# Sorting inside a graph network kernel: one vector product a step sooner, and two row-number operations moved between the halves of a one-hot matrix

## The chip, the cores and the metric

The kernel runs on one core of a Trainium2 chip, in one launch. The metric is the device time of an execution in microseconds (us). The core's engines work side by side, each through its own list of instructions in order: PE (matmuls, with PEld loading their weights), DVE (vector operations), ACT (activations and copies), POOL (here mostly indirect DMAs), and SP, which issues DMAs. An instruction that needs another engine's result waits on a semaphore, and all that stands behind it on its engine waits with it.

## The reference

A graph of 12,500 nodes with 64 features and 200,000 edges, sorted by destination. Two layers of neighbour means, then a network over the edges whose messages are averaged at the edge's source:

```
h = max(layernorm(x), 0)
for (Wl, Wr, b), relu in ((layer 1, yes), (layer 2, no)):
    agg  = segment_sum(h[src], dst)            # over 200,000 edges
    mean = agg / max(count(dst), 1)
    h    = mean @ Wl.T + b + h @ Wr.T          # relu after the first
x = x + h
h = max(layernorm(x), 0)
m = relu(concat(h[src], h[dst], edge) @ W1 + b1) @ W2 + b2
x = x + segment_sum(m, src) / max(count(src), 1)
```

## The kernel before, in words

The nodes are cut into 49 blocks of 256 (two nodes in each of 128 partitions). Every pair of a source block and a destination block is a cell, so there are 49 x 49 = 2401 cells with at most 128 edge slots each. Gathering and summing are matmuls with one-hot matrices, cell by cell. For that, the edges of every destination block have first to be sorted into their cells. This is the work of `sort(B)`, which is the place of the change.

**The sort of one block.** A block's window of edges lies as 128 partitions x 34 edges. `kv` says for each edge which source block it belongs to; `slo` and `dlo` are the local numbers (1 to 256) of its source and destination node inside their blocks. The sort runs in 13 steps (`STEPS = 13`; each `yield` ends one):

- step 1: DVE makes the one-hot matrix of source blocks, `v[:, :, 0]` (line 570, 1666 elements in each partition; the tile is called `hot3`, and `hot` in the profile).
- step 2: 34 small matmuls count the edges of each cell (line 575).
- step 3: DVE makes the running sums and `wide` (lines 579 to 582), and then comes the first of the four matmul steps.
- steps 4 to 6, with the rest of step 3, are a loop of four passes, n = 0 to 3: PE multiplies a piece of `v` (lines 591 and 592), and ACT copies the result into `ranks` (line 593). In passes 1 and 3 DVE also makes one product each (line 595): `v[:, :, 1]` = one-hot x `slo` in pass 1, and `v[:, :, 2]` = one-hot x `dlo` in pass 3. These products are the weights of the matmuls of line 619, four to five steps later.
- step 7: DVE takes minima over `ranks` (line 600 twice, line 603) and so gets each edge's rank in its cell, `rank`, and a rounded copy `rank_b` (line 605). Line 600 reads what ACT wrote in all four passes.
- steps 8 and 9: DVE makes the one-hot matrix of slots in two halves, `hot_r` (line 610, 2304 and 2048 elements in each partition).
- steps 10 and 11: PE multiplies the first half (18 matmuls) and the second half (16 matmuls) with the two products (line 619). Step 10 ends with two small DVE operations (lines 624 and 625, 34 elements in each partition) that work out `pos`, the rows of a table in memory to which POOL later scatters the edges' terms (line 370).
- steps 12 and 13: ACT copies the sums to `rows_o` (line 628); three DMAs write them out (lines 632 to 634), one of them to `srow_b`, which the layers read; PE and ACT turn them into `scol` and `dcol`.

**What runs around it.** The first block is sorted alone. From then on the steps of `sort` are dealt out between the groups of four cells of layer 1 (`sort_to`), about one step to a group once three blocks are ahead. A group gathers its cells (PE line 849, weights `turned`), copies them (ACT line 853, `rows`), and three groups later sums them (PE line 729, weights `hot`). DVE makes `turned` from `srow`, which SP loads, two operations to 16 cells (line 695), and one `hot` to a group (line 704, five buffers). At the end of each block's 49 cells comes `conv` (lines 770 to 794). From cell 150 on, the terms of the edges run beside it (`edge_terms`, lines 359 to 409, and POOL's scatter in line 370).

The order of instructions on each engine is that in which the Python code issues them; nothing reorders them. Tiles with one buffer are `v`, `wide`, `ranks`, `rank` and the bank `pX`; `kv`, `slo`, `dlo` and `hot_r` have two.

Of the kernel before, what the change touches and what calls it, by code (L numbers as in the profile page):

```python
# [9 lines left out]
FT = mybir.dt.float32  # L10
# [3 lines left out]
OP = mybir.AluOpType  # L14
AX = mybir.AxisListType
P = 128
# [98 lines left out]
def fast_path(  # L115
# [18 lines left out]
    nc = tc.nc  # L134
# [5 lines left out]
    NB = -(-N // BLK)  # L140
# [9 lines left out]
    T = 34  # L150
# [3 lines left out]
    S = P  # L154
# [14 lines left out]
    def table_of(B):  # L169

        if B < EARLY:
            return B % J, BJ, B // J
        i, j = divmod(B - EARLY, LJ)
        return J + j, len(range(j, LATE, LJ)), i
# [309 lines left out]
    def pos_of(B):  # L484
        return pos[:, B] if B < EARLY else pos_late[:, B - EARLY]
# [3 lines left out]
    def made_cells(work, psum):  # L489
# [61 lines left out]
        def pairs(a):  # L551
            return a.rearrange("p (g c) -> p g c", c=2)

        def mid(a, n):

            return a.unsqueeze(2).to_broadcast([a.shape[0], a.shape[1], n, 2])

        def lead_(a, n):

            return a.unsqueeze(1).to_broadcast([a.shape[0], n, a.shape[1], 2])  # L560

        def flat(a):
            return a.rearrange("p g k c -> p g (k c)")

        def sort(B):

            kv, slo, dlo = batch[B]

            v = work.tile([P, TG, 3, NB, 2], BF, name="hot3", bufs=1)
            nc.vector.tensor_tensor(v[:, :, 0], mid(pairs(kv), NB), lead_(kexp, TG), op=OP.is_equal)  # L570
            yield
            many = psum.tile([P, 512], FT, name="pX")
            for g in range(TG):
                for c in range(2):
                    nc.tensor.matmul(many[:NB, 2 * g + c:2 * g + c + 1], v[:, g, 0, :, c], ones[:, 0:1],  # L575
                                     start=True, stop=True)
            yield
            b = before[B % 2]
            nc.vector.tensor_tensor_scan(b[:, 1:T + 1], flat_ones, many[:NB, :T], 0.0, op0=OP.mult, op1=OP.add)
            w = work.tile([NB, TG, NB, 2], BF, name="wide", bufs=1)  # L580
            nc.vector.tensor_mul(w, mid(pairs(b[:, 0:T]), NB), lead_(own[:NB], TG))
            nc.vector.tensor_max(most, most, b[:, T:T + 1])


            r = work.tile([P, TG, NB, 2], BF, name="ranks", bufs=1)
            for n, g0 in enumerate(range(0, TG, 5)):
                yield
                g1 = min(g0 + 5, TG)
                p = psum.tile([P, 512], FT, name="pX")
                q = p[:, :(g1 - g0) * 2 * NB].rearrange("p (g k) -> p g k", k=2 * NB)  # L590
                nc.tensor.matmul(q, lead, flat(v[:, g0:g1, 0]), start=True, stop=False)
                nc.tensor.matmul(q, ones[:NB], flat(w[:, g0:g1]), start=False, stop=True)
                nc.scalar.copy(flat(r[:, g0:g1]), q)
                if n % 2:
                    nc.vector.tensor_mul(v[:, :, 1 + n // 2], v[:, :, 0], mid(pairs((slo, dlo)[n // 2]), NB))
            yield
            k = NB
            for _ in range(2):
                h = k - k // 2
                nc.vector.tensor_tensor(r[:, :, 0:k - h], r[:, :, 0:k - h], r[:, :, h:k], op=OP.min)  # L600
                k = h
            rank = work.tile([P, T], FT, name="rank", bufs=1)
            nc.vector.tensor_reduce(pairs(rank), r[:, :, 0:k].rearrange("p g k c -> p g c k"), AX.X, OP.min)
            rb = work.tile([P, T], BF, name="rank_b", bufs=1)
            nc.vector.tensor_scalar(rb, rank, float(S), None, op0=OP.add)
            halves = []
            for g0, g1 in ((0, (TG + 1) // 2), ((TG + 1) // 2, TG)):
                yield
                hot = work.tile([P, (TG + 1) // 2, S, 2], BF, name="hot_r")
                nc.vector.tensor_tensor(hot[:, :g1 - g0], mid(pairs(rb)[:, g0:g1], S), lead_(rexp, g1 - g0),  # L610
                                        op=OP.is_equal)
                halves.append((g0, g1, hot))
            p = psum.tile([P, 512], FT, name="pX")
            for g0, g1, hot in halves:
                yield

                for g in range(g0, g1):
                    for c in range(2):
                        nc.tensor.matmul(p[:2 * NB, :S], v[:, g, 1:3, :, c].rearrange("p v k -> p (v k)"),  # L619
                                         hot[:, g - g0, :, c], start=g + c == 0, stop=g + c == TG)  # L620
                if g0 == 0:
                    j, n, f = table_of(B)
                    q = work.tile([P, T], FT, name="pos_f", bufs=1)
                    nc.vector.scalar_tensor_tensor(q, rank, float(NB), kv, op0=OP.mult, op1=OP.add)
                    nc.vector.tensor_scalar(pos_of(B), q, float(n), float(n * (S * NB + NB) + f),
                                            op0=OP.mult, op1=OP.add)
            o = work.tile([2 * NB, S], BF, name="rows_o")
            nc.scalar.copy(o, p[:2 * NB, :S])
            yield
            n, f = place[B]  # L630
            F = len(order[n])
            nc.sync.dma_start(srow_b[B].rearrange("(k s) -> k s", s=S), o[0:NB])
            nc.sync.dma_start(srow_k[n][:, f * S:(f + 1) * S], o[0:NB])
            nc.sync.dma_start(drow_k[n][:, f * S:(f + 1) * S], o[NB:2 * NB])
            p = psum.tile([P, 512], FT, name="pX")
            pt = p.bitcast(BF)[:, 0:2 * NB]
            nc.tensor.transpose(pt, o, ident_b[:2 * NB, :2 * NB])
            nc.scalar.copy(scol[:, scol_at[n]:scol_at[n] + NB * F].rearrange("p (k f) -> p k f", f=F)[:, :, f],
                           pt[:, 0:NB])
            nc.scalar.copy(dcol[:, B * NB:(B + 1) * NB], pt[:, NB:])  # L640
            yield
# [4 lines left out]
        for B in range(NB):  # L646
            if B % CH == 3 and B + 4 < NB:
                coming = edges_in(B + 4, nc.sync)
            for _ in sort(B):
                next(coming, None)  # L650
                sorted_to[0] += 1
                yield
# [108 lines left out]
    work = layers.enter_context(tc.tile_pool(name="layers", bufs=2))  # L761
# [169 lines left out]
    work = ctx.enter_context(tc.tile_pool(name="last", bufs=2))  # L931
# [451 lines left out]
```

## Time and profile before

| what | value |
|---|---|
| median of 3 runs | 5045.93 us (5045.0 to 5051.07) |
| the profiled execution, its own time | 5056.79 us |
| its span, first to last instruction | 5055.0 us |
| mean granted clock of TensorE | 0.898 |
| first `ranks` to last `rows_o` (all sorting) | 121.8 to 1945.9 us of the span |
| 300 to 1950 us: PE / PEld / DVE / ACT / POOL busy | 1339.6 / 1146.2 / 978.7 / 716.9 / 913.4 us of 1650 |
| 300 to 1950 us: granted clock | 0.86 |
| 3600 to 4500 us: granted clock | 1.00 |

A group's row gives engine, line, operation, the tile written and the tiles read, the number of instructions, their time in sum and the mean of one in ns, and the engine's idle time before them with what ended it. In a timeline row come the start, the length, the engine and line, and in brackets how long the engine had been idle and what released it. "issue" is a wait for nothing that the profile shows. Four cells of a layer give eight matmuls each on lines 849 and 729.

### The profile page before, as it was taken

The numbers are of one execution on the slowest core, as the hardware profiler recorded it, in microseconds if no ns is written. First come the engines' busy times: TensorE is split into PE (matmuls) and PEld (weight loads), VectorE is DVE, ScalarE is ACT, GpSimd is POOL, SyncE is SP. The second block draws the span as 40 slices with busy tenths as digits, with TensorE's granted clock in tenths as the row PEclk, the third lists the DMA queues.
The fourth block names the chain that finished last, engine by engine and source line by source line (L and its number), as shares of the span: only waits on it lengthen the run. The fifth ranks groups of instructions, "written<-read, shape, count | busy, mean of one in ns | idle before, by whom it ended". The sixth has DMA issues, their size and how long they took to land.

```text
span 5055.0 us, 125955 instructions
## 1 busy us (share of the span) xinstructions
PE 4085.5 (81%) x50387; PEld 3709.4 (73%) x50387; DVE 3404.9 (67%) x5945; ACT 2592.5 (51%) x5894; POOL 2682.8 (53%) x2299
## 2 busy tenths in 40 slices
PE   0778887878878888787887787777899999999866
PEld 0666776666766776777777777776899999999865
DVE  5655655555655655555555555555899999999986
ACT  2333444444444444444454444444677777777643
POOL 2035555545655645544554454443577777776532
PEclk9888888888888888888899898888999999999987
DMA  8843222222222222322323222223566666665653
GB/s 304 300 150 97 79 71 76 66 72 76 74 75 79 81 70 81 98 83 91 93 92 96 88 91 89 85 92 92 195 199 207 196 193 191 199 189 183 185 157 96
DMA packets 382102, 635.58 MB, mean 126 GB/s; under 512 B 97555, under 2 KB 236951, under 8 KB 381425
## 3 DMA queue, kind: packets, MB, share of 16 engines
q1 hardware_dynamic: 318116, 572.31, 35.8%
q0 software_dynamic: 53312, 51.36, 3.5%
q8 instruction: 396, 6.49, 0.5%
q10 hardware_dynamic: 10076, 3.77, 0.3%
q14 instruction: 202, 1.65, 0.1%
HBM read 474.72 MB, written 155.83 MB: 125 GB/s over the span
## 4 chain that ended last, share of the span: by engine, by line
PE 62%; issue 11%; DVE 10%; ACT 5%; POOL 3%; DMA 3%; another core or an unknown queue 3%; SPq 1%; ACTq 1%; DVEq 0%; POOLq 0%
PE acc L729 21%; PE got L849 17%; PE got L1025 7%; PE pE L401 4%; PE got L1026 3%; PE pX L619 2%; DVE turned L695 2%; DVE turned_d L695 2%; POOL hidden L1036 2%; PE pE L389 2%; ACT rows L853 2%; DVE hot L704 1%; POOL terms L370 1%; PE pX L575 1%
## 5 line engine op out<-in xcount | busy, mean ns | idle before, releaser
L370 POOL DMA_INDIRECT terms<-terms_o,pos x1496 | 1697.7, 1135 | 1706.0 <-ACT terms_o L409 693.9
L853 ACT CAST rows<-got 128x384 bf16<-128x384 f32 x2402 | 1076.0, 488 | 1680.2 <-PE got L849 962.3
L729 PEld LDWEIGHTS <-hot 128*128 128x128 bf16 x12012 | 1113.6, 105 | 269.0 <-issue 229.6
L729 PE MATMUL acc<-rows,hot 128*128 128x193 bf16 x9604 | 1162.8, 265 | 119.9 <-issue 114.9
L849 PEld LDWEIGHTS <-turned 128*128 128x128 bf16 x9604 | 892.2, 104 | 295.4 <-issue 276.9
L1036 POOL TENSOR_TENSOR hidden<-hidden 128x512 f32<-128x512 f32 (+1 forms) x602 | 768.1, 1276 | 531.9 <-ACT hidden L1033 450.0
L695 DVE TENSOR_SCALAR turned<-srow,nid 128x2048 bf16<-128x2048 bf16 (+1 forms) x906 | 775.5, 870 | 239.7 <-PE got L849 116.4
L704 DVE TENSOR_TENSOR hot<-dcol,local 128x1024 bf16<-128x1024 bf16 x1202 | 807.3, 684 | 56.7 <-PE acc L729 23.5
L1025 PE MATMUL got<-tb,turned_d 128*128 128x128 bf16 x4802 | 753.4, 223 | 28.4 <-DVE turned_d L695 27.0
L1025 PE MATMUL got<-ta,turned 128*128 128x128 bf16 x4802 | 744.8, 223 | 20.4 <-DVE y L1030 13.1
L1026 PE MATMUL got<-tb,turned_d 128*128 128x64 bf16 x4802 | 685.3, 195 | 0.0
L1026 PE MATMUL got<-ta,turned 128*128 128x64 bf16 x4802 | 678.9, 195 | 0.0
L849 PE MATMUL got<-tb,turned 128*128 128x192 bf16 x4802 | 574.9, 262 | 109.7 <-issue 89.9
L849 PE MATMUL got<-ta,turned 128*128 128x192 bf16 x4802 | 577.5, 264 | 85.6 <-issue 74.4
L1044 ACT ACTIVATE hot_a<-every,less 128x256 bf16<-128x256 bf16 x1197 | 507.7, 496 | 0.0
L1025 PEld LDWEIGHTS <-turned_d 128*128 128x128 bf16 x4802 | 449.6, 100 | 38.0 <-DVE turned_d L695 37.3
L1025 PEld LDWEIGHTS <-turned 128*128 128x128 bf16 x4802 | 452.6, 100 | 8.2 <-issue 7.8
L1026 PEld LDWEIGHTS <-turned 128*128 128x128 bf16 x4802 | 446.0, 99 | 16.8 <-issue 15.3
L1026 PEld LDWEIGHTS <-turned_d 128*128 128x128 bf16 x4802 | 447.0, 99 | 0.0
L1033 ACT ACTIVATE hidden<-y 128x512 f32<-128x512 f32 (+1 forms) x301 | 190.1, 632 | 308.3 <-DVE y L1030 291.3
L1045 ACT ACTIVATE hot_a<-hot_a 128x1024 bf16<-128x1024 bf16 x300 | 316.9, 1056 | 9.5
L401 PE MATMUL pE<-we,edges_t 128*128 128x128 f32 x1666 | 291.4, 317 | 32.7 <-issue 30.3
(212 smaller groups left out, 5237.6 us busy)
## 6 DMA issues: line engine op xcount, KB each, us to landing
srow<-srow_b SPq DMA_DIRECT2D x300, 512.0 KB
srow<-srow_k SPq DMA_DIRECT2D x149, 512.0 KB
drow<-drow_k SPq DMA_DIRECT2D x149, 512.0 KB
terms<-tb SPq DMA_DIRECT2D x96, 704.0 KB
edges<-in_edge_attr_dram SPq DMA_DIRECT2D x235, 192.0 KB
terms_in<-terms SPq DMA_DIRECT2D x74, 352.0 KB
terms<-terms_o,pos POOLq DMA_INDIRECT x1496
sums_mem<-sums SPq DMA_DIRECT2D x49, 193.0 KB
```

Of the source, the lines that this page charges most:

```text
L370: nc.gpsimd.indirect_dma_start(out=terms[j][:], out_offset=bass.IndirectOffsetOnAxis(ap=pos_of(B)[:, t:t + 1], axis=0), in_=o[:, c, h], in ...
L401: nc.tensor.matmul(pm[:, c], et[:, c], we, start=True, stop=True)
L695: nc.vector.tensor_scalar(o[:, h, :n * S], r[:, :n * S], nid[:, h:h + 1], None, op0=OP.is_equal)
L704: nc.vector.tensor_tensor(o[:, :n], cols.rearrange("p (g c) -> p g c", c=2).unsqueeze(2).to_broadcast([P, n, 2 * P, 2]), local.rearrange(" ...
L729: nc.tensor.matmul(self.acc[B][:, h, :W3], lt, r[:, c, 0:W3], start=k + h == 0, stop=k == row - 1 and h == 1, skip_group_check=True)
L849: nc.tensor.matmul(p[:, (i - c) * D3:(i - c + 1) * D3], t[:, h, (a - c0 + i) * S:(a - c0 + i + 1) * S], table[:, (a + i) % NB, h], start=h ...
L853: nc.scalar.copy(g[:, c:c + m, :D3], p[:, :m * D3].rearrange("p (c d) -> p c d", c=m))
L1025: nc.tensor.matmul(p[:, c], lt, rt[:, 0:2 * D], start=i == 0, stop=False, skip_group_check=True)
L1026: nc.tensor.matmul(p[:, c, 0:D], lt, rt[:, 2 * D:], start=False, stop=i == 3, skip_group_check=True)
L1036: nc.gpsimd.tensor_sub(w[:, :n, (i + 1) * D:(i + 2) * D], w[:, :n, j], upper(w)[:, :n, j])
L1044: nc.scalar.activation(q[:, c - k], every, AF.Abs, bias=less[:, a - c0 + c:a - c0 + c + 1])
L1045: nc.scalar.activation(q[:, :n - k], q[:, :n - k], AF.Relu, bias=1.0, scale=-2.0)
```

## The change

Two edits in `sort`, both of which move DVE operations; the number, the shapes and the operands of the operations stay as they are.

```diff
                 nc.scalar.copy(flat(r[:, g0:g1]), q)
-                if n % 2:
-                    nc.vector.tensor_mul(v[:, :, 1 + n // 2], v[:, :, 0], mid(pairs((slo, dlo)[n // 2]), NB))
+                if n in (1, 2):
+                    nc.vector.tensor_mul(v[:, :, n], v[:, :, 0], mid(pairs((slo, dlo)[n - 1]), NB))
```

The product with `dlo` is issued in pass 2 instead of pass 3.

```diff
             for g0, g1 in ((0, (TG + 1) // 2), ((TG + 1) // 2, TG)):
                 yield
                 hot = work.tile([P, (TG + 1) // 2, S, 2], BF, name="hot_r")
                 nc.vector.tensor_tensor(hot[:, :g1 - g0], mid(pairs(rb)[:, g0:g1], S), lead_(rexp, g1 - g0),
                                         op=OP.is_equal)
                 halves.append((g0, g1, hot))
+                if g0 == 0:
+                    j, n, f = table_of(B)
+                    q = work.tile([P, T], FT, name="pos_f", bufs=1)
+                    nc.vector.scalar_tensor_tensor(q, rank, float(NB), kv, op0=OP.mult, op1=OP.add)
+                    nc.vector.tensor_scalar(pos_of(B), q, float(n), float(n * (S * NB + NB) + f),
+                                            op0=OP.mult, op1=OP.add)
             p = psum.tile([P, 512], FT, name="pX")
             for g0, g1, hot in halves:
                 yield

                 for g in range(g0, g1):
...
-                if g0 == 0:
-                    j, n, f = table_of(B)
-                    q = work.tile([P, T], FT, name="pos_f", bufs=1)
-                    nc.vector.scalar_tensor_tensor(q, rank, float(NB), kv, op0=OP.mult, op1=OP.add)
-                    nc.vector.tensor_scalar(pos_of(B), q, float(n), float(n * (S * NB + NB) + f),
-                                            op0=OP.mult, op1=OP.add)
```

The two row-number operations are issued in step 8, right behind the first half of `hot_r`, instead of at the end of step 10. In the changed kernel they are lines 616 and 617, and the matmuls of line 619 are line 625.

The order of PE, ACT, POOL and SP instructions is the same in both programs. On DVE the framework that places the semaphores puts 37 more separate waits in front of `hot` (line 704: 13 before, 50 after), each on a DVE operation ten or more instructions back; PE's weight loads for line 619 carry 9 waits fewer (12 before, 3 after).

## The prediction

> **What bounds the kernel now.** I read the page first, then the waits and the timeline of the stretch in which sorting runs.
>
> ```profile
> span 5055.0 us, 125955 instructions
> PE 4085.5 (81%) x50387; PEld 3709.4 (73%) x50387; DVE 3404.9 (67%) x5945; ACT 2592.5 (51%) x5894; POOL 2682.8 (53%) x2299
> PEclk9888888888888888888899898888999999999987
> PE 62%; issue 11%; DVE 10%; ACT 5%; POOL 3%; DMA 3%; another core or an unknown queue 3%; SPq 1%; ACTq 1%; DVEq 0%; POOLq 0%
> ```
>
> The chain that ended last is PE's for 62% and "issue" for 11%; the change touches DVE only. All of it lies between 117 and 1946 us, where a DVE operation costs time only if PE (or ACT, for PE) stands waiting for it. So I asked who waits, from 300 to 1950 us (columns: total us, times, longest):
>
> ```profile
> DVE ranks L600 <- ACT ranks L593: 87.2, 29, 7.6
> DVE ranks L600 <- ACT rows L853: 20.9, 9, 3.6
> DVE ranks L600 <- issue: 20.1, 5, 6.0
> PE pX L619 <- issue: 38.2, 68, 2.2
> PE pX L619 <- DVE hot_r L610: 2.0, 3, 1.2
> ```
>
> These 43 blocks make DVE stand 128 us in front of line 600, 3 us each: it has done its products long before ACT has copied the last ranks. PE, on its side, stands 2.0 us in total for the slots' matrix. The timeline of block 24 on DVE shows the order that the change rewrites:
>
> ```profile
> 1020.00 1.01 DVE L595 TENSOR_TENSOR hot<-hot,slo 128x1666 bf16<-128x1666 bf16 x1
> 1020.93 1.37 DVE L704 TENSOR_TENSOR hot<-dcol,local 128x1024 bf16<-128x1024 bf16 x2
> 1022.22 1.02 DVE L595 TENSOR_TENSOR hot<-hot,dlo 128x1666 bf16<-128x1666 bf16 x1
> 1024.23 0.75 DVE L695 TENSOR_SCALAR turned<-srow,nid 128x2048 bf16<-128x2048 bf16 x1 [0.99 <-PE got L849]
> 1024.90 0.68 DVE L704 TENSOR_TENSOR hot<-dcol,local 128x1024 bf16<-128x1024 bf16 x1
> 1027.04 0.99 DVE L600 TENSOR_TENSOR ranks<-ranks 128x816 bf16<-128x816 bf16 x2 [1.45 <-ACT ranks L593]
> ...
> 1031.72 2.49 DVE L610 TENSOR_TENSOR hot_r<-rank_b,rexp 128x2304 bf16<-128x2304 bf16 x2
> 1034.14 0.68 DVE L704 TENSOR_TENSOR hot<-dcol,local 128x1024 bf16<-128x1024 bf16 x1
> 1034.74 0.18 DVE L624 SCALAR_TENSOR_TENSOR pos_f<-rank,kv 128x34 f32<-128x34 f32 x1
> 1034.96 0.18 DVE L625 TENSOR_SCALAR pos<-pos_f 128x34 int32<-128x34 f32 x1
> 1035.05 0.69 DVE L704 TENSOR_TENSOR hot<-dcol,local 128x1024 bf16<-128x1024 bf16 x1
> ```
>
> **The product a step sooner.** One operation of 1.02 us in each of 49 blocks goes in front of up to two operations that stood before it, a `hot` or a `turned`. What it could win: line 600 starts sooner. It cannot, where DVE stands before it for ACT. Going through all 49 blocks, the first line 600 had an idle DVE in front of it in 48, and never less than 1.2 us. ACT's copies and PE's matmuls of those passes do not wait for the products, so line 600 stays and the idle time grows by the 1.02 us. The one block without idle time is block 4 (line 600 at 229.72). There line 605 ends at 231.57, the next operation is a `turned` that waits 3.46 us for the DMA of `srow` until 235.03, and swallows the 1.02. Gain: 0; bounds 0 to 1.02 us.
>
> What it could lose: the operations that now stand behind it come up to 1.02 us later. I took for each `hot` and `turned` between the two products the time from its end to the start of the first matmul that uses it. The smallest are 1.69, 1.71 and 2.42 us, all in block 4; the next is 4.9 us. A `hot` is summed three groups later, and that is the cover. All exceed 1.02, so the loss is 0. If the cover were gone, it would be 49 x 1.02 = 50 us.
>
> **The two row-number operations.** In a row of DVE work they take 1035.05 - 1034.74 = 0.31 us from the start of the first to the start of what follows. Alone they take more: in block 0 the first starts at 131.16 and the second, which waits for it, ends at 131.57, 0.41 us. I take 0.31, since the halves stand in a row with them, and keep 0.41 as the other end. In step 8 they push back the second half of `hot_r` and the groups' operations up to their old place. Cover of the second half: the time from its end to the first of its 16 matmuls. Over the 49 blocks this is 4.5 us in the median and below 0.41 us only in block 2 (end 172.33, matmuls at 172.40: 0.07 us); next come 0.47 (block 17) and 0.87 (blocks 0 and 1). So PE loses 0.31 - 0.07 = 0.24 us once, by the other end 0.34. The `turned` and `hot` in between have at least 1.08 us to their first matmul, more than 0.41. The operations behind the old place gain 0.31, and nobody waits for them. `pos` is ready sooner; the scatter that reads it waits for ACT's `terms_o` (429.8 us from 300 to 1950) and not for `pos`. Block 2's 0.24 us may vanish in the next wait for `srow`, so its bounds are 0 and 0.34.
>
> **Waits and queues.** SP, POOL, PE and ACT have the same order; no DMA is moved. The 37 added waits of DVE ask for DVE operations at least ten instructions old; the separate waits of line 704 in the trace last 21 ns each, together 0.8 us on an engine that idles 3 us a block in front of line 600. Behind such a wait stands the `hot` itself, with the slack above. Cost 0, bound 0.8.
>
> **Sum.** On the span of 5055.0 (execution 5056.79, so 1.79 outside): 0 + 0.24 + 0 = +0.2. That execution is 10.9 us over the median of the runs, so I add to the median: 5045.93 + 0.24 = 5046.2. Bounds of the costs: -1.0 (block 4) to +1.1 (0.34 + 0.8).
>
> A rule that speaks against this: in the profile the granted clock is 0.86 from 300 to 1950 us and 1.00 from 3600 to 4500, where PE is 96% busy. The Trainium skill, "TensorE: Matmul & The Clock Gate" (What's actually happening), says that the array drops to half clock after a quiet window of about 3.4 us, and that the windows run free. By the row, a PE wait of 0.24 us costs 0.24; by the rule it could tip a window and cost about 1.7 us more (an estimate, half of that page's 3.4). Either stays below what can be told.
>
> **Rivals.** *No change* (the forecast), 5046.2.
>
> *Slower: the second half becomes what PE waits for.* The place is the first matmul of step 11, the price 0.31 us a block, 49 x 0.31 = 15.2, so 5061 (by 0.41: 5066). It decides from the point where the second half's slack is below 0.31; for 10 us that must be so in 33 blocks. For it: PE stands for the first half (slack about 0.05 to 0.1) in 16 blocks, so DVE is late there, and the pair follows at once. Against it: a group of layer work separates the halves' matmuls, and only block 2 is that tight.
>
> *Faster: the slots' matrix comes sooner.* If line 600 were held by DVE's own work, the first half would be ready 1.02 us sooner. PE stands before it in 14 blocks: 3.69, 3.44, 0.76, 7.18, 2.17, 0.47, 0.03, 0.10, 1.21, 0.32, 0.54, 0.10, 0.10 and 1.18 us. Cut at 1.02 each, that is 8.5 us, so 5037. Against it: the idle time before line 600.
>
> *The stalls fall differently.* The clock of 0.86 takes 0.14 x 1650 = 231 us of full-clock time; "issue" stalls of PE lie in the same stretch. A shift of DVE by a microsecond can rearrange which loads meet which matmuls. A twentieth of 231 us is 12 us, either way: 5034 or 5058. For it: the stalls are large. Against it: the three runs agree within 6 us. *That the change does nothing on DVE* is out: the built order shows both moves.
>
> **How the numbers follow.** Within about 0.2% (10 us) two versions of this kernel can't be told apart. Forecast 0.60. Second half late 0.13. Slots' matrix sooner 0.07, of which 0.03 goes beyond 0.2% with help from the stalls. Stalls rearranged 0.20, of which I give 0.10 to faster, 0.09 to slower and 0.01 to the middle. So faster 0.13, same 0.60 + 0.04 + 0.01 = 0.65, slower 0.22. The likeliest case's own range is 5040 to 5052: its bounds and the 6 us spread of the runs. For 8 in 10 the range takes in the lighter rearrangements and most of the second-half case: 5034 to 5062.
>
> **What would show it.** In the profile after: the second product directly behind pass 2; DVE's idle time before line 600 up by about 1 us a block (154 us over all blocks before, some 200 after); the pair between the halves at 0.31 to 0.41 us; the second half's slack 0.3 to 0.4 us smaller while PE's idle time before its matmuls stays near nothing; granted clock 0.86 in the same stretch. I am wrong if PE stands before the second half in many blocks, if PE's waits for `hot` or `turned` rise from next to nothing, or if clock and "issue" between 300 and 1950 us differ by more than 10 us.

## The result, and the profile after

The changed kernel takes 5075.62 us (median of 20 runs, 5033.91 to 5119.84), beside 5048.43 us (5035.76 to 5075.13, 20 runs) for the kernel before. The ratio is 1.0052, with a 95% interval of 1.0031 to 1.0073; two runs of the changed kernel, 5111.3 and 5119.84 us, count as slow and are left out of it. It is slower by half a per cent, 27 us between the medians, and above the end of the predicted range. The profiled execution took 5091.81 us. On the page of the changed kernel (span, busy time by engine, granted clock in 40 slices, the chain that ended last):

```profile
span 5090.0 us, 125992 instructions
PE 4096.7 (80%) x50387; PEld 3720.7 (73%) x50387; DVE 3402.1 (67%) x5945; ACT 2584.0 (51%) x5894; POOL 2676.0 (53%) x2299
PEclk9878888888888888888988898898899999999987
PE 61%; issue 14%; DVE 9%; ACT 5%; POOL 4%; DMA 3%; another core or an unknown queue 3%; ACTq 1%; SPq 1%; POOLq 0%; DVEq 0%
```

The busy times are those of before, within some 11 us; the span is 35 us longer, "issue" in the chain went from 11% to 14%. So the change added waiting, not work. The waits of the changed kernel from 300 to 1950 us (total us, times, longest):

```profile
DVE ranks L600 <- ACT ranks L593: 73.6, 23, 6.7
DVE ranks L600 <- ACT rows L853: 26.8, 11, 3.6
DVE ranks L600 <- issue: 26.2, 7, 7.4
PE pX L625 <- issue: 36.4, 56, 2.2
```

DVE still stands in front of line 600 (126.6 us, 128.2 before), and PE's waits for `hot_r` are 1.5 us (2.0 before). The wait that the slower rival feared did not come. The timeline of DVE in block 24 of the changed kernel:

```profile
1036.26 1.01 DVE L595 TENSOR_TENSOR hot<-hot,slo 128x1666 bf16<-128x1666 bf16 x1
1037.20 0.68 DVE L704 TENSOR_TENSOR hot<-dcol,local 128x1024 bf16<-128x1024 bf16 x1
1037.80 1.01 DVE L595 TENSOR_TENSOR hot<-hot,dlo 128x1666 bf16<-128x1666 bf16 x1
1038.74 0.68 DVE L704 TENSOR_TENSOR hot<-dcol,local 128x1024 bf16<-128x1024 bf16 x1
1040.06 0.75 DVE L695 TENSOR_SCALAR turned<-srow,nid 128x2048 bf16<-128x2048 bf16 x1 [0.64 <-PE got L849]
...
1047.55 1.35 DVE L610 TENSOR_TENSOR hot_r<-rank_b,rexp 128x2304 bf16<-128x2304 bf16 x1
1048.82 0.19 DVE L616 SCALAR_TENSOR_TENSOR pos_f<-rank,kv 128x34 f32<-128x34 f32 x1
1049.05 0.18 DVE L617 TENSOR_SCALAR pos<-pos_f 128x34 int32<-128x34 f32 x1
1049.14 1.22 DVE L610 TENSOR_TENSOR hot_r<-rank_b,rexp 128x2048 bf16<-128x2048 bf16 x1
```

The second product has come forward past one `hot`, and the pair takes 1049.14 - 1048.82 = 0.32 us between the halves. What is worse is seen late in the sorting: in the windows from 1500 to 1950 us (busy time of PE, PEld, DVE, ACT and POOL with instructions, granted clock, DMA share, GB/s), first of before, then of after:

```profile
1500.00:1950.00 450.00, 368.50 (x3723) 319.57 (x3723) 275.56 (x524) 204.10 (x503) 260.25 (x213) 0.88 0.25 76
```

```profile
1500.00:1950.00 450.00, 364.45 (x3488) 310.60 (x3488) 260.70 (x493) 189.55 (x466) 236.01 (x200) 0.83 0.24 74
```

In equal time PE does 6% fewer matmuls at a lower clock, though the two windows do not hold quite the same work, since after is some 40 us behind by then. Compared at the same work, from line 570 of block 3 to that of block 48 the trace of before has 1737.8 us, with PE at half clock for 505 and idle for 344 us; after it is 1788.3 us, 584 and 366. All of the loss lies in the sorting stretch. The idle time that grew is the one called "issue": PE's gaps of over 0.15 us that end so sum up to 212.1 us in before and 238.4 in after, while those that ACT, DVE or a DMA ended did not grow. The profile alone does not say what sent PE there.

### The profile page after: what moved, and what is told of

Read it like the earlier page. It is cut to its first block, busy times and chain, and to the rows that moved or that the text cites. A ratio compares the mean times of both kernels' runs of the same rounds, so it can differ in the third digit from the quotient of the medians.

```text
span 5090.0 us, 125992 instructions
## 1 busy us (share of the span) xinstructions
PE 4096.7 (80%) x50387; PEld 3720.7 (73%) x50387; DVE 3402.1 (67%) x5945; ACT 2584.0 (51%) x5894; POOL 2676.0 (53%) x2299
## 4 chain that ended last, share of the span: by engine, by line
PE 61%; issue 14%; DVE 9%; ACT 5%; POOL 4%; DMA 3%; another core or an unknown queue 3%; ACTq 1%; SPq 1%; POOLq 0%; DVEq 0%
PE acc L729 21%; PE got L849 16%; PE got L1025 7%; PE pE L401 4%; PE got L1026 3%; PE pX L625 2%; POOL hidden L1036 2%; POOL terms L370 2%; DVE turned L695 2%; DVE turned_d L695 2%; PE pE L389 2%; ACT rows L853 2%; PE acc L792 1%; DMA srow<-srow_b 1%
## 5 line engine op out<-in xcount | busy, mean ns | idle before, releaser
L849 PE MATMUL got<-ta,turned 128*128 128x192 bf16 x4802 | 590.4, 266 | 114.3 <-issue 98.0
```

The lines of the kernel that those rows point to most:

```text
L849: nc.tensor.matmul(p[:, (i - c) * D3:(i - c + 1) * D3], t[:, h, (a - c0 + i) * S:(a - c0 + i + 1) * S], table[:, (a + i) % NB, h], start=h ...
```

## The experiments

The kernel before took 4141 to 4145 us in the jobs of e0 to e7 and of g1 to g3, 5042 us in that of e8 to e10, and 4900 us in that of f1 to f4; ratios are therefore always to the kernel before in the same job. The jobs ran on different chips (e0 to e7 on one, g1 to g3 on a second, e8 to e10 on a third, f1 to f4 on a fourth), so chip and job cannot be told apart as the reason. In e4, e5, e8 and f3 the lines from 595 on are three higher.

The theory called L in the expectations from e4 on came from POOL, whose scatters the prediction had not timed. The scatter of line 370 normally takes 0.97 us, but some take up to 7.8 us, and these lie across stretches in which DVE works without a break. So: a scatter can be held off until DVE stands idle; the product now fills a gap in which POOL got its turn. The main rival: the pair, or the rearranged waits that come with it. (Rival P in e4 to e9 is another: that PE or ACT waits for what the sooner product pushes back. Theory P in g2 and g3 is that at the slower level the loss is the pair's.)

### The parts alone: e0 to e3, and again g1 to g3

e0 is the kernel before, e3 and g1 the changed kernel. e2 and g2 take the second edit alone (the second hunk shown with the change), e1 and g3 the first alone:

```diff
-                if n % 2:
-                    nc.vector.tensor_mul(v[:, :, 1 + n // 2], v[:, :, 0], mid(pairs((slo, dlo)[n // 2]), NB))
+                if n in (1, 2):
+                    nc.vector.tensor_mul(v[:, :, n], v[:, :, 0], mid(pairs((slo, dlo)[n - 1]), NB))
```

> The kernel before once more, as a measure of what no change looks like. Every theory expects a ratio of 1.000 with an interval of about 0.2% either way; its runs should spread as before's 20 runs do (5036 to 5075 us). If this ratio is off by 0.3% or more, the 1.0052 of the changed kernel proves little.

> Only the second product a step sooner. Theory A (the row-number pair between the halves makes the loss): ratio 1.000, 5045 to 5052 us, DVE's idle time before line 600 up by 1 us a block. Theory B (the sooner product makes it, by delaying a layer operation or by an earlier start of the matmuls that it weights): ratio 1.004 to 1.006, some 5070 us. Theory C (both add up): about 1.0025 here and in the other half.

> Only the two row-number operations between the halves, with the 37 more waits on DVE that come with them. Theory A: ratio 1.004 to 1.006, some 5070 us, with more time at half clock between 300 and 1950 us than in the run of before (granted clock 0.84 against 0.86). Theory B: 1.000. Theory C: about 1.0025.

> The changed kernel once more, beside its two halves on one chip. If the loss is real: ratio 1.003 to 1.007, some 5070 us, with the wider spread of its 20 runs (5034 to 5120). If the first measurement was a matter of chance: 1.000 to 1.002.

> The changed kernel again. Where the kernel before takes 4141 us: 1.005 to 1.008, as e3. Where it takes 4900 us or more: 1.003 to 1.007 if the loss of 0.5% there is real, 0.998 to 1.002 if it was a chance of the runs.

> The row-number pair alone. At the faster level 0.998 to 1.000, as e2. At the slower level: theory P (there the loss is the pair's) 1.002 to 1.006; theory L (the product's at either level) 0.998 to 1.001; if neither part costs anything there, 0.998 to 1.002.

> The product a step sooner, alone. At the faster level 1.005 to 1.008, as e1. At the slower level: theory P 0.998 to 1.002, as f1; theory L 1.003 to 1.007.

| run | median us | ratio to before, 95% interval |
|---|---|---|
| e0 unchanged | 4140.49 | 0.9995 [0.9986, 1.0003] |
| e1 product alone | 4170.59 | 1.0063 [1.0049, 1.0076] |
| e2 pair alone | 4136.75 | 0.9989 [0.9981, 0.9998] |
| e3 both | 4171.05 | 1.0065 [1.0053, 1.0077] |
| g1 both | 4165.06 | 1.0046 [1.0032, 1.0061] |
| g2 pair alone | 4137.02 | 0.9977 [0.9967, 0.9988] |
| g3 product alone | 4175.90 | 1.0068 [1.0054, 1.0083] |

In this table the product carries the whole loss, twice; the pair, and the 37 waits that come with it, win 0.1 to 0.2%. How it comes about is seen in block 44. The timeline of e0 (the kernel before), DVE and then POOL:

```profile
1405.16 1.28 DVE L704 TENSOR_TENSOR hot<-dcol,local 128x1024 bf16<-128x1024 bf16 x2
1406.37 1.01 DVE L595 TENSOR_TENSOR hot<-hot,slo 128x1666 bf16<-128x1666 bf16 x1
1407.30 0.68 DVE L704 TENSOR_TENSOR hot<-dcol,local 128x1024 bf16<-128x1024 bf16 x1
1408.69 0.75 DVE L695 TENSOR_SCALAR turned<-srow,nid 128x2048 bf16<-128x2048 bf16 x1 [0.71 <-PE got L849]
1409.36 0.68 DVE L704 TENSOR_TENSOR hot<-dcol,local 128x1024 bf16<-128x1024 bf16 x1
1409.96 1.02 DVE L595 TENSOR_TENSOR hot<-hot,dlo 128x1666 bf16<-128x1666 bf16 x1
```

```profile
1405.47 3.35 POOL L370 DMA_INDIRECT terms<-terms_o,pos  x1 [0.30 <-issue]
```

DVE stops at 1407.98, because the next `turned` waits 0.71 us for PE. The scatter that began at 1405.47 ends at 1408.82, 0.84 us after DVE stopped: almost its normal 0.97 us, so by its length nearly all of its work was done only then. The same place in e1, DVE first, then what follows on all engines:

```profile
1428.16 1.28 DVE L704 TENSOR_TENSOR hot<-dcol,local 128x1024 bf16<-128x1024 bf16 x2
1429.36 1.01 DVE L595 TENSOR_TENSOR hot<-hot,slo 128x1666 bf16<-128x1666 bf16 x1
1430.30 0.67 DVE L704 TENSOR_TENSOR hot<-dcol,local 128x1024 bf16<-128x1024 bf16 x1
1430.90 1.01 DVE L595 TENSOR_TENSOR hot<-hot,dlo 128x1666 bf16<-128x1666 bf16 x1
1431.84 0.74 DVE L695 TENSOR_SCALAR turned<-srow,nid 128x2048 bf16<-128x2048 bf16 x1
1432.50 0.67 DVE L704 TENSOR_TENSOR hot<-dcol,local 128x1024 bf16<-128x1024 bf16 x1
1433.10 0.73 DVE L695 TENSOR_SCALAR turned<-srow,nid 128x2048 bf16<-128x2048 bf16 x1
1433.76 0.67 DVE L704 TENSOR_TENSOR hot<-dcol,local 128x1024 bf16<-128x1024 bf16 x1
```

```profile
1427.47 7.81 POOL L370 DMA_INDIRECT terms<-terms_o,pos  x1 [0.30 <-issue]
...
1439.13 0.59 ACT L409 COPY terms_o<-pE 128x512 f32<-128x512 f32 x1 [6.36 <-DMA terms<-terms_o,pos]
...
1439.76 0.47 PE L389 MATMUL pE<-ident,edges 128*128 128x128 f32 x1 [5.64 <-ACT terms_o L409]
```

The product now stands where DVE used to wait, the run of DVE goes on to 1434.43, and the scatter ends at 1435.28, again 0.85 us after it. Then the cost travels: ACT waits 6.36 us for a free `terms_o` buffer, which the scatters empty, and PE waits 5.64 us for ACT. In block 25, where the run was unbroken before, the scatter takes 7.81 us in e0 and 7.82 in e1.

Summed from the traces, from line 570 of block 6 to that of block 48 (about 725 scatters):

| run | stretch us | sum of the scatters us | scatters over 6 us |
|---|---|---|---|
| e0 unchanged | 1221.3 | 996.8 | 14 |
| e2 pair | 1216.4 | 993.9 | 11 |
| e1 product | 1250.7 | 1026.7 | 23 |
| e3 both | 1249.9 | 1025.1 | 19 |
| e4 one break (below) | 1174.9 | 947.1 | 0 |
| e5 two breaks (below) | 1148.3 | 922.6 | 0 |

From e0 to e1 the stretch grows by 29.4 us and the scatters by 29.9: the loss in time and the lengthening of the scatters are of one size. The longest unbroken run of DVE in a block, between 12 us ahead of its first product and its line 600, is 8.4 us in the mean of e0 and 9.3 us in e1 (blocks 6 to 47; idle times under 0.1 us are not counted as breaks).

The blocks can be told apart. In e0 DVE stands idle between the two products in only 9 of the blocks 6 to 47 (12 to 14, 28 to 30 and 44 to 46), 4.7 us in all; in e1 it does so in none. The time of the blocks, line 570 to line 570, with the product in its old place and a step sooner, from one trace of each run (e6 and e7, without scatters, come below):

| pair of traces | the 9 blocks, us | the other 33, us |
|---|---|---|
| e0 and e1 | 260.0, then 289.2 | 961.3, then 961.5 |
| e2 and e3 (both with the pair) | 259.7, then 289.3 | 956.7, then 960.7 |
| e6 and e7 (both without scatters) | 236.7, then 236.7 | 881.1, then 880.8 |

The loss of e1 lies wholly in the blocks whose gap was closed, and there alone the scatters got longer: their sum went from 207.9 to 238.9 us in the 9 blocks and from 788.9 to 787.8 in the others. In g3 it is 283.2 us and, in the other 33, 969.7, so there 8 us of the loss against e0 lie outside.

Not all DVE work holds a scatter. Of the 39 scatters of e0 in this stretch that take over 3 us, 38 lie across one of the products of line 595 and none across lines 600 to 610; of the 651 that touch no product, mostly under DVE work too, one takes over 3 us. Which property of an operation counts was not separated.

### No scatters: e6 and e7

In e6 the call that issues the scatter is taken out of the kernel before; e7 is the same with the product a step sooner.

```diff
-                    nc.gpsimd.indirect_dma_start(
-                        out=terms[j][:], out_offset=bass.IndirectOffsetOnAxis(
...
```

> The kernel before without the 1666 scatters of the edges' terms (line 370), so the terms stay zero and the output lacks them. Both theories: faster than before by some per cent, since POOL no longer holds the terms' buffers. It is the base for the next kernel.

> The same without the scatters, with the second product a step sooner. Theory L: no scatter, no loss: within 0.15% of the kernel without scatters and with the product in its old place. Rival P: the loss of 0.6% stays, some 25 us.

3966.75 us, 0.958 [0.9565, 0.9595], and 3967.5 us, 0.9586 [0.9569, 0.9602]. Without scatters the earlier product costs 0.02% by the medians and 0.06% by the ratios, inside the intervals; with them it cost 0.63%. The same 9 gaps are closed in e7, and their blocks take 236.7 us as in e6 (table above). So the loss at this level goes through the scatters.

### A wait put in on purpose: e4 and e5

The changed kernel, with a one-element copy ahead of the second product that reads what ACT wrote in this pass, so that DVE must stand there until ACT has copied. In e5 the copy stands ahead of both products.

```diff
                 if n in (1, 2):
+                    if n in (2,):
+                        late = work.tile([P, 1], BF, name="late")
+                        nc.vector.tensor_copy(late, r[:, g1 - 1, NB - 1, 1:2])
                     nc.vector.tensor_mul(v[:, :, n], v[:, :, 0], mid(pairs((slo, dlo)[n - 1]), NB))
```

> The changed kernel with one DVE operation more in each block: in pass 2, ahead of the product with dlo, one element in each partition is copied from what ACT has just written, so that DVE has to stand there until ACT is done. Theory L (POOL's scatter can't go on while DVE works without a break, and the sooner product closed a break): the break is back, the loss goes although work and a wait are added: ratio 0.996 to 1.001, and scatters longer than 6 us nearly vanish. Rival P (PE or ACT wait for what the sooner product pushes back): it is pushed back further, so 1.006 or more.

> As the kernel with one break, and the same break ahead of the product with slo in pass 1 too. Theory L: the runs of DVE work are cut once more, so the scatters' time falls below that of the kernel before: ratio 0.985 to 0.995. Rival P: 1.007 or more.

4095.77 us, 0.9895 [0.9876, 0.9913], and 4061.49 us, 0.9813 [0.9798, 0.9828]. Both gain more than was expected, and both are faster than either kernel. DVE and POOL in block 44 of e4:

```profile
1358.10 1.28 DVE L707 TENSOR_TENSOR hot<-dcol,local 128x1024 bf16<-128x1024 bf16 x2
1359.30 1.01 DVE L598 TENSOR_TENSOR hot<-hot,slo 128x1666 bf16<-128x1666 bf16 x1
1360.24 0.67 DVE L707 TENSOR_TENSOR hot<-dcol,local 128x1024 bf16<-128x1024 bf16 x1
1365.52 0.16 DVE L597 COPY late<-ranks 128x1 bf16<-128x1 bf16 x1 [4.61 <-ACT ranks L593]
1365.59 1.02 DVE L598 TENSOR_TENSOR hot<-hot,dlo 128x1666 bf16<-128x1666 bf16 x1
```

```profile
1357.41 4.35 POOL L370 DMA_INDIRECT terms<-terms_o,pos  x1 [0.30 <-issue]
1362.06 0.97 POOL L370 DMA_INDIRECT terms<-terms_o,pos  x1 [0.30 <-ACT rows L856]
1363.33 0.97 POOL L370 DMA_INDIRECT terms<-terms_o,pos  x1 [0.30 <-issue]
1364.61 0.97 POOL L370 DMA_INDIRECT terms<-terms_o,pos  x1 [0.30 <-issue]
```

DVE gives up 4.61 us that it did not need, and POOL runs three scatters of 0.97 us in it; the held one ends 0.85 us after DVE's last operation (1360.91). The list of all scatters by shape gives the shortest, median and longest in ns, of e1 and then of e5:

```profile
L370 POOL DMA_INDIRECT terms<-terms_o,pos x1496: 964/1026/7823, 291.5 to 2647.3; - x187
```

```profile
L370 POOL DMA_INDIRECT terms<-terms_o,pos x1496: 964/1049/3750, 288.8 to 2546.7; - x187
```

The medians are 2% apart; the long tail is gone. In the table above, e4 and e5 win 75.0 and 101.6 us of the stretch against e3, and their scatters 78.0 and 102.5 us.

### Is it the wait or the operation: e8

The copy as in e4, but from `slo`, which has long been there, so that nothing is waited for.

```diff
-                        nc.vector.tensor_copy(late, r[:, g1 - 1, NB - 1, 1:2])
+                        nc.vector.tensor_copy(late, slo[:, 0:1])
```

> The changed kernel with the same one-element copy ahead of the product with dlo, but from slo, which has long been there, so that DVE has one operation more and no wait. Theory L in its plain form (POOL gets its turn when DVE stands idle): ratio 1.004 to 1.008, and scatters over 6 us as often as in the changed kernel. Variant M (a DVE operation with one small input is a gap too): the loss goes, 0.988 to 1.001. If the breaks had helped for another reason than the wait, by delaying the product for instance, this kernel would stay at 1.005 too, but then the scatters' long times would not go with the total.

5063.62 us, 1.0041 [1.0008, 1.0073]: as theory L expected, and 7 scatters from block 6 to 48 are over 6 us, as in the trace of after. But the kernel before took 5041.65 us here, and at such a level the product alone shows no cost (f1 below), so the time does not decide; the trace does. A long run of e8 in block 25, DVE around the copy, and the scatter that begins at 1073.12:

```profile
1076.61 0.68 DVE L707 TENSOR_TENSOR hot<-dcol,local 128x1024 bf16<-128x1024 bf16 x1
1077.21 0.14 DVE L597 COPY late<-slo 128x1 bf16<-128x1 bf16 x1
1077.28 1.00 DVE L598 TENSOR_TENSOR hot<-hot,dlo 128x1666 bf16<-128x1666 bf16 x1
```

```profile
1073.12 7.88 POOL L370 DMA_INDIRECT terms<-terms_o,pos  x1 [0.30 <-issue]
```

The scatter lies across the copy, 0.14 us long, and is not let in. Beside e4, where the same copy waits, it is the standing still that counts and not one operation more. How long DVE has to stand was not varied.

### Other places, and other levels of speed: e9, e10 and f1 to f4

e9 and f4 put both products into pass 1 and the pair back to its old place (first diff); e10 is the changed kernel with breaks ahead of step 1 and in passes 0, 1 and 2 (second diff). f1, f2 and f3 are e1, e2 and e5 again.

```diff
+                if n == 1:
+                    for m, lo in ((1, slo), (2, dlo)):
+                        nc.vector.tensor_mul(v[:, :, m], v[:, :, 0], mid(pairs(lo), NB))
```

```diff
+            if B:
+                late = work.tile([P, 1], BF, name="late")
+                nc.vector.tensor_copy(late, dcol[:, B * NB - 1:B * NB])
             nc.vector.tensor_tensor(v[:, :, 0], mid(pairs(kv), NB), lead_(kexp, TG), op=OP.is_equal)
...
                 nc.scalar.copy(flat(r[:, g0:g1]), q)
+                if n < 3:
+                    late = work.tile([P, 1], BF, name="late")
+                    nc.vector.tensor_copy(late, r[:, g1 - 1, NB - 1, 1:2])
```

> The kernel before, with both products one behind the other in pass 1. The run of DVE work that begins with step 3 always holds both then. Theory L: at least the loss of the sooner product, ratio 1.006 to 1.012, with more time in scatters over 6 us than the sooner product alone. Rival P (what waits for PE and DVE alone counts): the two products are ready sooner and the layer's operations have the same slack less 1 us, 0.999 to 1.002.

> The kernel with the two breaks, with two more: in pass 0, and in step 1 ahead of the one-hot matrix (there DVE waits for ACT's dcol of the block before). Theory L: the scatters get shorter again, ratio 0.972 to 0.981. It fails to gain where DVE itself gets late by its waits: then 0.981 to 0.99, and PE's waits for hot_r grow beyond the 27 us that they have with two breaks.

> The kernel before with the product a step sooner, alone. Theory L (the product fills an idle gap of DVE in which POOL's scatter used to get its turn): 1.004 to 1.008 at either level of speed, and most of the changed kernel's 1.0052. Rival R (at the slower level, where POOL is busy only 53% of the stretch, the 0.5% comes from rearranged stalls of PE's feed and is not the product's own): 0.998 to 1.002 at the slower level.

> The kernel before with the row-number pair between the halves, alone. Theory L: 0.998 to 1.000. Rival R: at the slower level as large as the product's part, 1.002 to 1.006 (the two parts share the loss in any way).

> The changed kernel with a one-element copy from ACT's ranks ahead of both products, so that DVE waits there. Theory L: 0.978 to 0.990 of the time before at either level. Rival R: at the slower level the breaks win little, 0.994 to 1.004.

> The kernel before with both products in pass 1. Theory L: where the run of DVE operations after pass 1 grows by the second product as it does in pass 2, 1.004 to 1.010. Rival G (what counts is not the product's place as such but whether a wait of DVE for PE or ACT is left behind it before the next scatter is due; in pass 1 one is left): 0.998 to 1.003.

| run | before us | this us | ratio, 95% interval |
|---|---|---|---|
| e9 both in pass 1 | 5041.65 | 5048.13 | 1.0010 [0.9982, 1.0038] |
| e10 four breaks | 5041.65 | 4967.04 | 0.9867 [0.9829, 0.9906] |
| f1 product | 4900.09 | 4906.21 | 1.0004 [0.9978, 1.0030] |
| f2 pair | 4900.09 | 4926.08 | 1.0036 [1.0002, 1.0070] |
| f3 two breaks | 4900.09 | 4812.30 | 0.9813 [0.9774, 0.9851] |
| f4 both in pass 1 | 4900.09 | 4901.51 | 1.0003 [0.9977, 1.0029] |

Here theory L missed: f1, e9 and f4 cost nothing that can be told, where it expected a loss, and f2 is above its range. Rival R, rearranged stalls of PE, has both f1 and f2 in its ranges, and f3 outside; rival P has e9 in its range, rival G f4. The pair's 1.0036 is at the edge of its interval and without a mechanism in its trace (from line 570 of block 3 to that of block 48 the profiled f2 takes 1682.4 us, f1 1686.3). Only the breaks hold at every level. e10 gained less than f3 and less than its first range; its expectation put that down to PE's waits for `hot_r`, which were to grow beyond 27 us. They did not (from 300 to 1950 us; 20.9 us in f3):

```profile
PE pX L631 <- DVE hot_r L616: 20.6, 11, 3.6
```

Where the kernel takes 4900 us or more, POOL is not what PE follows. In the trace of before it waits for ACT (429.8 us for `terms_o` from 300 to 1950 us), while in e0 from 300 to 1600 no such wait is among POOL's; the longest run of DVE is shorter (6.6 us in the mean over blocks 6 to 47 in before, 6.9 in after; 8.4 and 9.3 in e0 and e1); and the sums of the scatters of before and after in that stretch are 898.4 and 884.8 us, with 7 over 6 us in each. In the 19 of the blocks 6 to 47 in which after has less idle time between the products than before, the scatters do grow, by 17.3 us, and these blocks by 15.4. But the other 23 blocks, where no gap was closed, grow by 35.0 us while their scatters shrink by 30.9. So most of the loss between these two profiles does not go the way that e0 and e1 show.

## Why the prediction was wrong

**The step that failed.** The prediction says of a DVE operation that it "costs time only if PE (or ACT, for PE) stands waiting for it". It went through everyone that waits for DVE by a semaphore, priced the product at 0 by their slack, took the gaps of DVE as free, and left PE's "issue" stalls and the clock out of the sum. In the comparison that it forecast, the loss stands in what was left out: PE's "issue" idle time is 26 us longer and its half clock 79 us, while PE's waits for ACT, DVE and DMAs did not grow. Which edit did it there, and how, is open (below).

**The product a step sooner, costed at 0 (0 to 1.02 us won, 0 lost by slack).** At 4141 to 4145 us this term is measured, and wrong. Its reading of idle time was: "ACT's copies and PE's matmuls of those passes do not wait for the products, so line 600 stays and the idle time grows by the 1.02 us". But POOL's scatter gets on when DVE stands still, and it is held inside the instruction, where no semaphore shows it. The product costs 0.63 and 0.68% (e1, g3), the scatters take 29.9 us more, the loss of e1 lies in the 9 blocks whose gap it closed, and without scatters the cost is gone (e7). Line 370 was named in the prediction, but only for `pos` and `terms_o`; the length of its instructions, 967 to 7801 ns in the trace of before, was not read. The forecast of the idle time was off too: in front of line 600 it went from 154.5 to 161.2 us over all blocks, not to some 200. Between the products of blocks 6 to 47 it went from 25.2 us in 24 gaps to 3.6 in 6.

**A rule that was missed.** The Trainium skill has it in "SBUF — State Buffer" (SBUF: two separate sides, with the warning on the "DVE blocks DMA" trap and A bandwidth-pool intuition that's wrong; and Who interferes with whom): DVE and GpSimd, here POOL, share a port pair as an exclusive lock; while DVE holds it, in a two-port mode, POOL can't write the descriptors of a DMA that it issues. The trace agrees that some scatters are held while DVE works. The page gives an end of the blocking some 115 ns after DVE's end, and a lock that is held for one instruction. Here a scatter is held across eleven DVE instructions in a row (e1), and held ones end 0.84 to 0.86 us after the last (block 44 of e0, e1 and e4; in e8, block 25, 1081.00 - 1080.14 = 0.86); when the blocking itself ends, the trace does not show. Most of these instructions are TENSOR_TENSOR, and the trace does not tell in which mode they ran. That it is this lock is the skill's reading; the runs show the dependence on DVE's runs, not the port.

**The pair, 0.24 us.** Its mechanism is seen in the trace: 0.32 us in block 24 beside the 0.31 used, and the second half's slack shrank to 0.05 us in block 2. PE's idle time ahead of the second half is 0.13 us there, and at most 0.47 in any block (27). At 4141 to 4145 us the pair alone takes 0.9989 and 0.9977; at 4900 us it takes 1.0036, and why is not known. The rival of the late second half, 15.2 us, did not come.

**Waits, 0.** Right at 4141 to 4145 us: all 37 come with e2 and g2, which lost nothing. They come with f2 too.

**The stalls fall differently, 5034 or 5058.** This rival came nearest to what the first profile shows: half clock up by 79 us and PE idle by 23 in sorting, and clock and "issue" beyond the 10 us named as a sign of error. It named both directions, so its sign was no forecast, and its size, a twentieth of 231 us or 12 us, was a guess without a mechanism: the medians lie 27 us apart. The spread of 6 us, which made the range, was that of three runs; the 20 runs of before lie 39 us apart.

**What stays open.** Why the first comparison lost 0.52%. At 4141 to 4145 us the way through the scatters is shown. In the first comparison it may stand behind the 15.4 us of the 19 blocks; for the other 35.0 us no run shows a cause. At 4900 us the product alone shows no cost within 0.3%, the pair perhaps one, and both together were not run there. At 5042 us the changed kernel with an idle copy has 1.0041, and the kernel with both products in pass 1 and the pair in its old place 1.0010. That the pair carries the loss there fits all of these and is not shown. Also open is what the breaks win where POOL is not the bound: in f3, from block 3 to block 48, PE's "issue" idle time (gaps over 0.15 us) is 112.1 us, beside 209.1 in f1 and 182.8 in f4, and half clock 345 us beside 413 and 440.

## What to carry to other kernels

Idle time of DVE was not free here, where POOL issues indirect DMAs: before a DVE operation is moved into a gap, list how long POOL's transfers take and lay the long ones over DVE's unbroken runs. A deliberate wait can pay: tiny DVE operations that wait for another engine, ahead of work that nobody needs soon, won 1.9% here at both levels at which this was tried, where work moved forward into the gaps cost up to 0.7%. Slack against semaphores is only half of a proof that a move is free. Comparing the blocks that a change touched with those that it left alone, trace against trace, showed here what the totals could not.

## What the runs showed of the hardware that was not expected

- A scatter of 0.97 us stretches to 7.88 us across eleven and more back-to-back DVE operations, and ends 0.84 to 0.86 us after DVE falls idle in the cases shown. Most under a run are not held: of the 350 scatters of e0 (blocks 6 to 47) that began with at least 3 us of a DVE run still to come, 313 took under 2 us. In e4 one that began at 1354.12 took 1.44 us.
- A DVE copy of one element and 0.14 us in the middle of such a run did not let the scatter in (e8, block 25); a wait of 4.61 us did (e4, block 44).
- The same program takes 4141 to 4145, 4900 or 5042 to 5048 us in different jobs on different chips, and a part of a change can be worth 0.6% in one and nothing that can be told in another. From block 3 to 48, PE's "issue" idle time (gaps over 0.15 us) is 212.1 us in the first profile of before and none in e0; why is not known.
